# A sparse graph attention kernel: q and softmax weights in columns of their own of two PSUM banks, weights and weighted values one group later

## The chip, the core and the metric

The kernel runs on one core of one Trainium2 chip. Five engines work side by side: TensorE (PE) multiplies matrices and writes only to PSUM, VectorE (DVE) does elementwise work and reductions, ScalarE (ACT) copies and applies functions, GpSimd (POOL) here issues the gathers and takes powers, and SyncE (SP) issues plain DMAs. Each engine runs its own instructions in the program's order and waits on semaphores where it needs another engine's result.

The metric is the device time of the whole kernel in microseconds. The time before is 2392.24 us, the median of three runs from 2391.94 to 2392.58.

## The reference, cut to what matters

Four graph layers over 3327 nodes with 256 features. The adjacency matrix is given densely (3327 x 3327 integers), but a node has only about 16 neighbours. Layer 0 is a small graph attention over the dense matrix. Layers 1 to 3 are alike, each with its own weights: attention of 8 heads over a node's neighbours, then a feed-forward part.

```python
def layer(x, adj, w_qkv, w_proj, b_proj, w1, b1, w2, b2, g1, be1, g2, be2):
    qkv = (layer_norm(x, g1, be1) @ w_qkv).reshape(n, 3, HEADS, HEAD_DIM)
    q, k, v = qkv[:, 0], qkv[:, 1], qkv[:, 2]
    scores = jnp.einsum('nhd,mhd->hnm', q, k) * SCALE
    scores = jnp.where((adj != 0)[None], scores, -jnp.inf)
    attn = jax.nn.softmax(scores, axis=-1)
    out = jnp.einsum('hnm,mhd->nhd', attn, v).reshape(n, DIM)
    x = x + out @ w_proj + b_proj
    ff = jax.nn.gelu(layer_norm(x, g2, be2) @ w1 + b1) @ w2 + b2
    return x + ff
# x = layer 0 of x; then this layer three times, with L1, L2 and L3's weights
```

## The kernel before

**Stages.** The first stage computes layer 0 and, beside it, a list of neighbours for every node. It also sorts the nodes by their number of neighbours, so that a block of 128 nodes has lists of nearly one length. There are 26 blocks; `CAPS` gives each block's list length, from 34 for block 0 down to 9 for block 25. The three attention layers follow. They are written by one function, `layer(L)`, and the order in which instructions stand in each engine's queue is the order of that Python code (`tc.manual_schedule()`).

**A block.** Blocks go through attention in the order 24, 23, ..., 1, 0, 25 (`ORDER`). A block's list is cut into groups of three or four neighbours (`cuts`), so that a block has 3 to 9 groups and a layer 118 groups with 430 neighbours in all. One object of the class `Attend` stands for a block in a layer:

- `gather(g)` (L764) lets GpSimd issue one indirect DMA for each neighbour of a group. It brings the k and v rows of 128 nodes into a slot; there are 12 slots, taken in turn.
- `load_q` (L753) loads the block's q from DRAM through SP's queue (layers 2 and 3), and `place_q` (L757) lets ScalarE copy it into a PSUM tile, `qp`.
- `scores(g)` multiplies the slot's k by q (L778) and sums over each head's 32 columns (L779), both on VectorE.
- `exps` stands after the block's last group: mask and maximum (L785 to L788) on VectorE, and the exponential (L789) on ScalarE.
- `shares` sums the exponentials and inverts the sum (L795, L796), and writes the normalised weights (L799) over q's columns of the same tile `qp`.
- `values(g)` multiplies the slot's v by the weights (L811). TensorE then transposes the products and adds them up in PSUM (L814); after the last group ScalarE copies the result to `oT` (L820).

**The order of the loop.** The loop of `layer` runs over blocks, and within them over groups. In each step it issues gathers up to three groups ahead, this block's scores, one `turn()` of the tails, and then the weighted values of the *block before*: its `shares` in the first group and its groups spread so that they are done one group before this block ends. When the last is done, `place_q` of the next block is issued. It comes so late because q and the weights of a block share columns, and because there are two `qp` tiles: the tile for the next block is the one whose weights have just been used up.

**Tails.** Two blocks together (one for the last two) make a chunk. When a chunk's values are done, a generator `tail` is added to a list, and each `turn()` lets every generator take its next step. A tail is the projection (`pp`, L665) and its residual add (L668), a norm (variance on VectorE, the power L137 on GpSimd, L149 on VectorE, L153 on ScalarE), the transposed input `fT` (L163, L165), the feed-forward in two halves (`pu` L689, gelu L693, `pd` L702), the second residual add (L708), another norm, and the next layer's q, k and v (L183 to L190), which SP writes to DRAM. In the last layer the rows are scattered to the output instead (L713). The list `hidden` lets one tail at a time through its feed-forward.

The tiles `fT` and `hT` of all tails share two buffers. The next layer's gathers can start only when all rows of k and v have been written, so each layer ends with its tails running out while no gather is under way.

Of the kernel before, what the change touches and what calls it, by code (L numbers as in the profile page):

```python
# [8 lines left out]
FP = mybir.dt.float32  # L9
# [6 lines left out]
PSUM = bass.MemoryType.PSUM  # L16
DRAM = bass.MemoryType.DRAM

P = 128
N = 3327  # L20
D = 256
HEADS = 8
# [9 lines left out]
NB = (N + P - 1) // P  # L32
# [10 lines left out]
LW = 40  # L43
# [21 lines left out]
def kernel(ctx: ExitStack, tc: tile.TileContext, ins, out: bass.AP):  # L65
# [563 lines left out]
    with ExitStack() as st:  # L629
# [3 lines left out]
        slots = st.enter_context(tc.tile_pool(name="slots", bufs=SLOTS))  # L633
        ps_g = st.enter_context(tc.tile_pool(name="ps2_g", bufs=4, space=PSUM))
        ps_o = st.enter_context(tc.tile_pool(name="ps2_o", bufs=2, space=PSUM))
        ps_q = st.enter_context(tc.tile_pool(name="ps2_q", bufs=2, space=PSUM))

        def gen(name):
            return ps_g.tile([P, 512], FP, tag="g", name=name)

        x_sb = keep.tile([P, NB, D], FP, name="x_sb")
        def node_x(b):
            nc.scalar.copy(x_sb[:, b, :], nodes_[b][:, :D])

# [7 lines left out]
        def tail(L, w, wqn, blocks, oT):  # L652
# [19 lines left out]
            yield AHEAD - 1  # L672
            xns = normed(work, views, mv, rs, f"f{tag}")
            yield 1
            fT = work.tile([P, 2, 2 * P], FP, tag="fT", name=f"fT_{tag}")
            turned(gen, fT, xns, *gains(L, 1), f"f{tag}")
            yield 1
            pd = None
            while hidden:
                yield 1  # L680
            hidden.append(tag)
            for h in range(2):
                gT = work.tile([P, FH, 2 * P], FP, tag="gT", name=f"gT_{tag}_{h}")
                for f0 in range(0, FH, 2):
# [54 lines left out]
        class Attend:  # L739


            def __init__(self, L, b):
                self.L, self.b, self.tag, self.S = L, b, f"{L}_{b}", CAPS[b]
                self.cuts = cuts(b)
                self.tiles = []
                self.vdone = 0

            def load_q(self):
                if self.L == LAYERS[0]:
# [3 lines left out]
                    nc.sync.dma_start(self.q, q_dr[self.L][:, self.b, :])  # L753

            def place_q(self):
                self.qp = ps_q.tile([P, 512], FP, tag="qp", name=f"qp_{self.tag}")
                nc.scalar.copy(self.qp[:, :D], self.q)  # L757

            def gather(self, g):
                a, z = self.cuts[g]  # L760
# [8 lines left out]
            def scores(self, g):  # L769
                a, z = self.cuts[g]  # L770
                n = z - a
                if g == 0:
                    self.sc = work.tile([P, LW, HEADS], FP, tag="sc", name=f"sc_{self.tag}")
                if self.L == LAYERS[0]:

                    nc.scalar.copy(idx[:, self.b, a:z], self.tiles[g][:, :n, 2 * D])
                kq = self.tiles[g][:, :n, :D]
                nc.vector.tensor_mul(kq, kq, self.qp[:, None, :D].to_broadcast([P, n, D]))  # L778
                nc.vector.tensor_reduce(self.sc[:, a:z, :],  # L779
                                        kq.rearrange("p s (h d) -> p s h d", h=HEADS), AX.X, ALU.add)  # L780

# [9 lines left out]
            def shares(self):  # L791
                S = self.S
                scs = self.sc[:, :S, :]
                sm = work.tile([P, HEADS], FP, tag="sm", name=f"sm_{self.tag}")
                nc.vector.tensor_reduce(sm, scs.rearrange("p s h -> p h s"), AX.X, ALU.add)  # L795
                nc.vector.reciprocal(sm, sm)  # L796

                self.pw = self.qp[:, :LW * HEADS].rearrange("p (s h) -> p s h", h=HEADS)
                nc.vector.tensor_mul(self.pw[:, :S, :], scs, sm[:, None, :].to_broadcast([P, S, HEADS]))  # L799
                self.po = ps_o.tile([P, 2, P], FP, tag="po", name=f"po_{self.tag}")  # L800
                nc.tensor.matmul(self.po.rearrange("p c r -> p (c r)"), zeros_bf[:, :P], zeros_bf,
                                 start=True, stop=False)
# [24 lines left out]
        def turn():  # L827

            for e in list(tails):
                e[0] -= 1  # L830
                if e[0] <= 0:
                    e[0] = next(e[1], None)
                    if e[0] is None:
                        tails.remove(e)

        def layer(L):
            w = load_weights(L)
            wqn = load_wq(L + 1) if L < LAYERS[-1] else None
            att = [Attend(L, b) for b in ORDER]
            todo = [(a, g) for a in att for g in range(len(a.cuts))]  # L840
            turns = len(todo)
            held = 0
            sent = 0
            oTs = {}
            left = [len(c) for c in CHUNKS]
            first = L == LAYERS[0]
            if first:
                for b in ORDER[:EARLY]:
                    node_rows(b)
                    node_x(b)  # L850
            att[0].load_q()
            att[0].place_q()
            att[1].load_q()
            before = None

            def part(a):

                m, j = place[a.b]
                if m not in oTs:
                    oTs[m] = work.tile([P, 2, 2 * P], FP, tag="oT", name=f"oT_{L}_{m}")  # L860
                if a.values(oTs[m], j):
                    left[m] -= 1
                    if not left[m]:
                        tails.append([1, tail(L, w, wqn, CHUNKS[m], oTs.pop(m))])

            now = 0
            for k, a in enumerate(att):
                n = len(a.cuts)
                if k + 2 < NB:
                    att[k + 2].load_q()  # L870
                for g in range(n):
                    if first and g == 0:
                        if k + EARLY < NB:
                            node_rows(ORDER[k + EARLY])
                        if EARLY <= k + 2 < NB:
                            node_list(ORDER[k + 2])
                            node_x(ORDER[k + 2])
                    while sent < turns and held < SLOTS and sent - now <= AHEAD:
                        todo[sent][0].gather(todo[sent][1])
                        sent += 1  # L880
                        held += 1
                    a.scores(g)
                    if g == n - 1:
                        a.exps()
                    turn()
                    if k == NB - 1:
                        turn()
                    if before is not None:
                        if g == 0:
                            before.shares()  # L890
                        goal = max(g + 1, -(-len(before.cuts) * (g + 1) // max(n - 1, 1)))
                        while before.vdone < min(goal, len(before.cuts)):
                            part(before)
                            held -= 1
                            if before.vdone == len(before.cuts) and k + 1 < NB:
                                att[k + 1].place_q()
                    elif g == n - 1:
                        att[1].place_q()
                    now += 1
                before = a  # L900
            before.shares()
            while before.vdone < len(before.cuts):
                part(before)
                turn()
            while tails:
                turn()
# [194 lines left out]
```

## Time and profile before

| what | value |
|---|---|
| median of the runs | 2392.24 us |
| profiled execution | 2871.28 us |
| its span, first to last instruction | 2869.2 us |
| mean granted TensorE clock in it | 0.753 |
| busy: PE, DVE, ACT, POOL | 1716.9, 1756.5, 776.2, 1430.0 us |
| layer 0 and lists, up to the first gather | 411.2 us |
| layer 1, first to last gather | 773.8 us |
| end of layer 1, to the next gather | 77.0 us |
| layer 2, first to last gather | 725.4 us |
| end of layer 2 | 79.2 us |
| layer 3, first to last gather | 734.9 us |
| end of layer 3, to the end | 67.6 us |

A profile shows one execution. In this case it took 479 us longer than the runs without the profiler, so a wait in it isn't at once a wait of the timed runs. In the groups of the page, each line has the source line, the engine, the operation, the tiles written and read, how often; then the busy time and the mean duration, and after the second bar the time for which the engine stood idle just before these instructions, with what ended most of it. "remote" and "another core or an unknown queue" mean that the profile can't name what ended a wait. In a timeline, each row has a start and a duration in us, the engine, the line and the operation, and in brackets the idle time before it.

### The profile page before, as it was taken

Reading aid. Unit: us, or ns where it says so; the run is one execution under the profiler, and the core shown is the slowest. Engines: PE = TensorE matmul, PEld = TensorE weight load, DVE = VectorE, ACT = ScalarE, POOL = GpSimd, SP = SyncE. Lnnn points to the kernel's source line nnn. Section 1 sums busy time; section 2 is a strip of 40 time slices with the busy share of each in tenths; the row PEclk is TensorE's granted clock in tenths of the full one; section 3 lists DMA queues with packets and bytes.
Section 4 is the critical chain, followed back from the end, with each engine's and each line's share of the span. In section 5 each row is a group of like instructions: output and inputs, shape, how many; then the busy total and the mean of one; then the engine's idle time right before and its main releaser. Section 6 shows DMA issues by size and latency. Waiting matters only on the chain.

```text
span 2869.2 us, 26077 instructions
## 1 busy us (share of the span) xinstructions
PE 1716.9 (60%) x8346; PEld 1327.7 (46%) x8346; DVE 1756.5 (61%) x3214; ACT 776.2 (27%) x1564; POOL 1430.0 (50%) x1614
## 2 busy tenths in 40 slices
PE   7677622455666666752576676666725555566556
PEld 6555411444454444642454555554514444444445
DVE  5777735665667776725565755767246467555664
ACT  4777510123322222220232222122302222111112
POOL 0232345554456665336555556664165555665561
PEclk9889855677877667885687777777957777676768
DMA  5667155555456665345545556565255555555451
GB/s 211 218 179 223 59 137 165 151 172 148 129 156 187 178 183 169 109 154 170 148 146 158 174 162 191 169 182 151 99 175 161 155 152 155 168 172 152 145 170 30
DMA packets 165082, 453.04 MB, mean 158 GB/s; under 512 B 37711, under 2 KB 64985, under 8 KB 161609
## 3 DMA queue, kind: packets, MB, share of 16 engines
q0 software_dynamic: 107104, 350.26, 41.8%
q1 hardware_dynamic: 56652, 98.53, 10.9%
q10 hardware_dynamic: 1180, 2.49, 0.3%
q8 instruction: 69, 1.13, 0.2%
q14 instruction: 77, 0.63, 0.1%
HBM read 410.86 MB, written 40.29 MB: 157 GB/s over the span
## 4 chain that ended last, share of the span: by engine, by line
PE 32%; another core or an unknown queue 18%; DVE 17%; issue 15%; ACT 6%; POOL 6%; DMA 5%; DVEq 0%; ACTq 0%; SPq 0%; POOLq 0%
PE pd L702 8%; PE pu L689 7%; PE po L814 5%; PE pk L183 4%; DVE sl L778 4%; DVE sl L811 4%; POOL sl L764 3%; PE pp L665 3%; DVE sc L779 2%; DMA kv<-kvr 2%; DMA sl<-kv,idx 2%; PE pq L188 2%; ACT gT L693 1%; ACT L693 1%
## 5 line engine op out<-in xcount | busy, mean ns | idle before, releaser
L764 POOL DMA_INDIRECT sl<-kv,idx x1290 | 1229.0, 953 | 544.0 <-issue 355.4
L814 PE MATMUL po<-ident,sl 128*128 128x128 f32 x2580 | 471.7, 346 | 568.1 <-DVE sl L811 302.4
L778 DVE TENSOR_TENSOR sl<-sl,qp 128x1024 f32<-128x1024 f32 (+1 forms) x354 | 396.3, 1119 | 568.4 <-ACT qp L757 484.3
L814 PEld LDWEIGHTS po<-ident,sl 128*128 128x128 f32 x2580 | 395.6, 180 | 634.2 <-DVE sl L811 360.3
L702 PE MATMUL pd<-w,gT 128*128 128x256 f32 x1248 | 336.1, 427 | 165.4 <-ACT gT L693 112.6
L779 DVE TENSOR_REDUCE sc<-sl 128x32 f32<-128x1024 f32 (+1 forms) x354 | 398.2, 1125 | 29.5 <-remote 10.5
L689 PE MATMUL pu<-fT,w 128*128 128x256 f32 (+1 forms) x1344 | 328.6, 402 | 127.9 <-issue 66.4
L811 DVE TENSOR_TENSOR sl<-sl,qp 128x1024 f32<-128x1024 f32 (+1 forms) x354 | 388.9, 1119 | 8.1 <-DVE qp L799 3.5
L702 PEld LDWEIGHTS pd<-w,gT 128*128 128x128 f32 x1248 | 261.2, 215 | 228.0 <-ACT gT L693 127.1
L689 PEld LDWEIGHTS pu<-fT,w 128*128 128x128 f32 x1344 | 266.0, 213 | 176.2 <-issue 72.3
L693 ACT ACTIVATE gT<-pu,pv 128x256 f32<-128x256 f32 (+1 forms) x336 | 133.1, 456 | 374.5 <-remote 175.3
L137 POOL TENSOR_TENSOR rsig_f<-rsig_f,mhalf 128x2 f32<-128x2 f32 (+1 forms) x42 | 29.1, 693 | 339.6 <-DVE rsig_f L133 337.6
L820 ACT COPY oT<-po 128x256 f32<-128x256 f32 x78 | 29.1, 373 | 617.3 <-remote 228.6
L183 PE MATMUL pk<-wq,hT 128*128 128x512 f32 x312 | 169.6, 670 | 19.8 <-ACT hT L165 18.6
L708 DVE TENSOR_TENSOR x_sb<-x_sb,pd 128x512 f32<-128x512 f32 (+1 forms) x42 | 27.2, 648 | 207.2 <-PE pd L702 144.9
L608 DVE MAX8 cand<-abf 128x8 f32<-128x256 bf16 x338 | 118.2, 411 | 1.3 <-DMA node<-cand 1.1
L665 PE MATMUL pp<-w_proj,oT 128*128 128x256 f32 x312 | 94.1, 452 | 35.6 <-ACT oT L820 26.3
L165 ACT ACTIVATE fT<-pn_f,pv 128x256 f32<-128x256 f32 (+1 forms) x84 | 41.6, 545 | 249.2 <-remote 155.1
L693 ACT ACT_TABLE_LOAD x48 | 61.6, 1283 | 151.9 <-remote 88.4
L183 PEld LDWEIGHTS pk<-wq,hT 128*128 128x128 f32 x312 | 61.6, 215 | 71.8 <-issue 42.6
L185 ACT COPY kvr<-pk 128x512 f32<-128x512 f32 x78 | 46.0, 589 | 180.5 <-PE pk L183 125.5
L137 POOL TENSOR_TENSOR rsig_h<-rsig_h,mhalf 128x2 f32<-128x2 f32 (+1 forms) x28 | 19.5, 695 | 146.3 <-DVE rsig_h L133 118.2
(220 smaller groups left out, 1999.7 us busy)
## 6 DMA issues: line engine op xcount, KB each, us to landing
a<-in_adj_dram SPq DMA_DIRECT2D x25, 1663.5 KB
sl<-kv,idx POOLq DMA_INDIRECT x1290
kv<-kvr SPq DMA_DIRECT2D x78, 256.0 KB
q<-qr SPq DMA_DIRECT2D x52, 128.0 KB
q<-q SPq DMA_DIRECT2D x52, 128.0 KB
w<-in_L_gnn_w_dram SPq DMA_DIRECT2D x6, 1024.0 KB
node<-x SPq DMA_DIRECT2D x26, 128.0 KB
node<-qr SPq DMA_DIRECT2D x26, 128.0 KB
```

The lines of the kernel that those rows point to most:

```text
L183: nc.tensor.matmul(pk, hT[:, c, :], wq[:, c, D:], start=(c == 0), stop=(c == 1))
L188: nc.tensor.matmul(pq[:, :D], hT[:, c, :], wq[:, c, :D], start=(c == 0), stop=(c == 1))
L608: nc.vector.max(out=cand[:, 8 * m:8 * m + 8], in_=ab3[:, m, :])
L665: nc.tensor.matmul(pp[:, j, :], oT[:, c, j * P:(j + 1) * P], w["w_proj"][:, c, :], start=False, stop=(c == 1 and j == n - 1))
L689: nc.tensor.matmul(pu[:, a, :n * P], w["w1"][:, c, f * P:(f + 1) * P], fT[:, c, :n * P], start=(c == 0), stop=(c == 1))
L693: nc.scalar.activation(gT[:, f0 + a, :n * P], pu[:, a, :n * P], AF.Gelu_apprx_tanh, bias=pv[:, L - 1, 8 + f:9 + f])
L702: nc.tensor.matmul(pd[:, j, :], gT[:, f, j * P:(j + 1) * P], w["w2"][:, h * FH + f, :], start=False, stop=(h == 1 and f == FH - 1 and j == ...
L764: nc.gpsimd.indirect_dma_start(out=t[:, k - a, :w], out_offset=None, in_=kv_dr[self.L][:, :], in_offset=bass.IndirectOffsetOnAxis(ap=idx[: ...
L778: nc.vector.tensor_mul(kq, kq, self.qp[:, None, :D].to_broadcast([P, n, D]))
L779: nc.vector.tensor_reduce(self.sc[:, a:z, :], kq.rearrange("p s (h d) -> p s h d", h=HEADS), AX.X, ALU.add)
L811: nc.vector.tensor_mul(vv, vv, self.pw[:, a:z, :, None].to_broadcast([P, n, HEADS, HD]))
L814: nc.tensor.matmul(self.po[:, c, :], t[:, k, D + c * P:D + (c + 1) * P], ident, is_transpose=True, start=False, stop=(a + k == self.S - 1 ...
```

## The change

There are four edits, which belong together.

1. The two `qp` tiles from a pool become two fixed tiles, `qws`, one PSUM bank each. A block uses one by its place in the order, even or odd. Its q has the first 256 columns and its weights have the last 256 (272 for block 0, whose weights then overlap q's last 16 columns).
2. `place_q` of the block after the next is issued right behind this block's exponentials. The first two blocks' q are placed before the loop.
3. `shares` and `values` of the block before start in the second group of a block, not the first, and end in its last.
4. In `tail`, the wait for `hidden` stands ahead of the making of `fT`, not behind it.

```diff
-        ps_q = st.enter_context(tc.tile_pool(name="ps2_q", bufs=2, space=PSUM))
+        ps_q = st.enter_context(tc.tile_pool(name="ps2_q", bufs=1, space=PSUM))
...
+        qws = [ps_q.tile([P, 512], FP, name=f"qw{k}") for k in range(2)]
...
             xns = normed(work, views, mv, rs, f"f{tag}")
             yield 1
+            while hidden:
+                yield 1
+            hidden.append(tag)
             fT = work.tile([P, 2, 2 * P], FP, tag="fT", name=f"fT_{tag}")
             turned(gen, fT, xns, *gains(L, 1), f"f{tag}")
             yield 1
             pd = None
-            while hidden:
-                yield 1
-            hidden.append(tag)
...
+                w = qws[ORDER.index(b) % 2]
+                self.qp = w[:, :D]
+                self.pw = w[:, 512 - max(D, self.S * HEADS):512].rearrange("p (s h) -> p s h", h=HEADS)
...
             def place_q(self):
-                self.qp = ps_q.tile([P, 512], FP, tag="qp", name=f"qp_{self.tag}")
-                nc.scalar.copy(self.qp[:, :D], self.q)
+                nc.scalar.copy(self.qp, self.q)
...
-                self.pw = self.qp[:, :LW * HEADS].rearrange("p (s h) -> p s h", h=HEADS)
...
             att[1].load_q()
+            att[1].place_q()
...
                     if g == n - 1:
                         a.exps()
+                        if k + 2 < NB:
+                            att[k + 2].place_q()
                     turn()
                     if k == NB - 1:
                         turn()
-                    if before is not None:
-                        if g == 0:
+                    if before is not None and g > 0:
+                        if g == 1:
                             before.shares()
-                        goal = max(g + 1, -(-len(before.cuts) * (g + 1) // max(n - 1, 1)))
+                        goal = max(g, -(-len(before.cuts) * g // (n - 1)))
                         while before.vdone < min(goal, len(before.cuts)):
                             part(before)
                             held -= 1
-                            if before.vdone == len(before.cuts) and k + 1 < NB:
-                                att[k + 1].place_q()
-                    elif g == n - 1:
-                        att[1].place_q()
```

More of the change, by code (lines that the diff above doesn't have):

```diff
@@ L777, in scores @@
                 kq = self.tiles[g][:, :n, :D]
-                nc.vector.tensor_mul(kq, kq, self.qp[:, None, :D].to_broadcast([P, n, D]))
+                nc.vector.tensor_mul(kq, kq, self.qp[:, None, :].to_broadcast([P, n, D]))
                 nc.vector.tensor_reduce(self.sc[:, a:z, :],
```

## The prediction

> **What bounds the kernel now.** I read the times first: the profiled execution took 2871.3 us (span 2869.2), the median without the profiler is 2392.2. The profile is 479 us too long, so before anything is priced I must know what these 479 us are. Then the page's chain and groups, the table by stage, the timeline around the longest wait, and the end of a layer.
>
> The page's chain by engine, and its groups with the gather and the three large VectorE products:
>
> ```profile
> PE 32%; another core or an unknown queue 18%; DVE 17%; issue 15%; ACT 6%; POOL 6%; DMA 5%; DVEq 0%; ACTq 0%; SPq 0%; POOLq 0%
> ...
> L764 POOL DMA_INDIRECT sl<-kv,idx x1290 | 1229.0, 953 | 544.0 <-issue 355.4
> ...
> L778 DVE TENSOR_TENSOR sl<-sl,qp 128x1024 f32<-128x1024 f32 (+1 forms) x354 | 396.3, 1119 | 568.4 <-ACT qp L757 484.3
> L779 DVE TENSOR_REDUCE sc<-sl 128x32 f32<-128x1024 f32 (+1 forms) x354 | 398.2, 1125 | 29.5 <-remote 10.5
> ...
> L811 DVE TENSOR_TENSOR sl<-sl,qp 128x1024 f32<-128x1024 f32 (+1 forms) x354 | 388.9, 1119 | 8.1 <-DVE qp L799 3.5
> ```
>
> The wait that the change goes for is the 484.3 us in the L778 line: VectorE stands until ScalarE has copied the next q into PSUM. It has almost the size of the 479 us, so the timeline of ScalarE, VectorE and GpSimd around one such wait:
>
> ```profile
> 1530.27 1.28 ACT L693 ACT_TABLE_LOAD   x1
> 1547.24 1.57 ACT L693 ACTIVATE gT<-pu,pv 128x256 f32<-128x256 f32 x4 [15.68 <-remote]
> 1548.68 0.39 ACT L820 COPY oT<-po 128x256 f32<-128x256 f32 x1
> 1548.93 0.42 ACT L757 COPY qp<-q 128x256 f32<-128x256 f32 x1
> ...
> 1549.38 1.22 DVE L778 TENSOR_TENSOR sl<-sl,qp 128x1024 f32<-128x1024 f32 x1 [17.05 <-ACT qp L757]
> ...
> 1542.55 0.96 POOL L764 DMA_INDIRECT sl<-kv,idx  x1 [0.30 <-issue]
> 1558.92 0.71 POOL L137 TENSOR_TENSOR rsig_f<-rsig_f,mhalf 128x2 f32<-128x2 f32 x1 [15.42 <-DVE rsig_f L133]
> ```
>
> The q copy (L757) stands behind the copy of the finished rows (L820), and that behind gelus which wait 15.68 us for TensorE. Yet TensorE's rows put the matmuls they wait for at 1528.9 to 1534. Such late signals come about once for each pair of blocks while gathers run; between 1180 and 1290, where they pause, no matmul's signal is over 1 us late. Down the line GpSimd stands 15.42 us at L137 and the gathers with it.
>
> The table by stage (us; busy time of PE, PEld, DVE, ACT, POOL): layer 1, its end, layer 2.
>
> ```profile
> 411.20:1185.00 773.80, 441.13 (x1864) 337.89 (x1864) 507.61 (x963) 179.96 (x479) 445.11 (x473) 0.72 0.56 165
> 1185.00:1262.00 77.00, 64.55 (x330) 48.47 (x330) 31.23 (x61) 28.18 (x68) 4.57 (x7) 0.93 0.13 42
> 1262.00:1987.50 725.50, 441.85 (x1864) 339.11 (x1864) 448.43 (x633) 159.28 (x317) 424.39 (x452) 0.74 0.59 175
> ```
>
> Now GpSimd's sum. Gathers that follow without a wait start every 1.257 us (0.95 busy, 0.30 to the next). The three layers last 773.8, 725.4 and 734.9 us from first to last gather: 2234.1. In them GpSimd must do 3 x 429 steps of 1.257 = 1617.8; 55 powers (L137) of 0.71 with a 0.19 gap = 50; 22 row gathers of layer 1 (L199) at 1.25 = 28; 22 output scatters of layer 3 at 1.3 plus the 22.7 us that they wait for each other's landing = 51. Together 1746, so in the profile it stands 488 us. Without them the profiled execution would take 2871 - 488 = 2383 us, 9 below the median. My reading: in the timed runs the late signals are mostly gone and **GpSimd's gather queue sets the pace inside the layers**; VectorE (448 of 725 us busy in layer 2) follows with room. The 484 us are mainly the profiler's.
>
> **What the Trainium skill says.** "Perfetto Trace Analysis", section "Tensor Engine Instruction (MATMUL, LD_WEIGHTS)": a matmul's reported end is computed from its size, the signal comes later. The trace agrees: end at 1534, gelus at 1547.24. "DMA: Bandwidth & Descriptors", section "SWDGE vs HWDGE vs iDMA": descriptors of irregular DMAs are computed by software on GpSimd; this agrees with a gather that costs 0.95 us of that engine whoever waits, and I take its price to be the same without the profiler. "PSUM — Partial Sum Buffer", section "Terms": two engines may not use one bank at once, so q's copy and the weights of one bank have to be ordered even in separate columns; the trace only shows copy and product in turn. "ScalarE: Activation LUTs", section "Terms": a table load is about 2.7 us; here it is 1.28 (L789, L693), and the trace decides.
>
> **The change part by part.**
>
> *q placed earlier.* The 78 copies of 0.38 us stay. Each moves from behind the last weighted values (and L820) of the block before to right behind the exponentials, one block earlier than it is read. L778 then never waits for TensorE by way of L820. The new cover is a whole block, 12 us for the smallest. On SP the q load stays at the block's start; in layers 2 and 3 it must land before the copy at the block's end, or ScalarE's later gelus stand behind it; 28.7 us of such waits in 2 cases now. I take 0, bound 0 to +10.
>
> *Weights one group later.* L795, L796, L799 (0.36 + 0.20 + 0.30) wait for the exponential, which may have a 1.28 us table load ahead; with one more group of scores (2.4 us) between, that is covered. If TensorE is late, nothing of this helps L668 and L708, the residual adds (91.5 and 144.9 us of waits in the profile): they are next.
>
> *Values one group later.* Same products, same transposes. A slot is held one group (5 us) longer. A gather's slot is that of 12 groups before; with blocks of 6 groups its values come 7 groups after its scores, so 4 groups remain: 0, bound +5.
>
> *Where VectorE's delay counts.* Inside layers only the 9 us. At the end of a layer its lateness is on the path: the first group of the last block of layer 1 is scored 12 us after its last gather is issued, at the layer's start it is 4, so 8 us are late, 3 x 8 = 24 with three layers. 9 + 24 = 33 us at most; I take 30.
>
> *What the layer's end loses.* There the tails run one after another:
>
> ```profile
> 1225.71 0.69 DVE L708 TENSOR_TENSOR x_sb<-x_sb,pd 128x512 f32<-128x512 f32 x1 [7.84 <-PE pd L702]
> ...
> 1240.48 0.42 DVE L708 TENSOR_TENSOR x_sb<-x_sb,pd 128x256 f32<-128x256 f32 x1 [10.32 <-PE pd L702]
> ...
> 1250.72 0.42 DVE L708 TENSOR_TENSOR x_sb<-x_sb,pd 128x256 f32<-128x256 f32 x1 [8.04 <-PE pd L702]
> ```
>
> Three feed-forwards follow each other, then the kv rows are written and the next layer's gather starts at 1262.07. With values one group later each starts later. Of the last pair, the 32 transposes of four groups (3.66 us) now lie between its first pu and pd, where they ended before pu; pu itself starts some 2 us earlier, so +1.6. The next block's L149 comes behind the last block's L668 and statistics (0.42 + 0.43 + 0.18 + 0.15 = 1.2). And fT is now made after the place is free (`hidden`): a transpose of 0.38 and an activation of 0.81, +1.2. That is +4; where VectorE is not late, the whole group of 5 us shows and it is about +10. I take 6 a layer: +18.
>
> Sum: 2392.2 - 30 + 18 = **2380 us**. In the profiled execution more can come off, as late signals no longer reach VectorE by L757; that is not in the timed runs.
>
> **The rivals.**
> 1. *Much faster: the queue has more room than I think.* If the 0.30 us gap is 0.19 without the profiler (the gap after L137), the queue needs 1290 x 0.11 = 142 us less and stands that much for VectorE. L757's share of VectorE's waits is 484 of some 820 us; 59% of 142 is 84, half of it 42; with the 18 back, 2392 - 42 + 18 = 2368, with all 2326; I put it at 2345. For it: the size of the wait. Against: the 2383 fit the median almost by themselves.
> 2. *Slower: the layer's end.* VectorE isn't late in the timed runs, nothing is won there, and each end costs 6 to 10 us: +18 to +30, less up to 9 won inside: 2412. One place (TensorE's order between last gather and first of the next layer), one price, and it decides as soon as less than 18 us are won. For it: the gathers need no VectorE that is faster. Against: the lags of 12 us.
> 3. *The wait only moves.* The copy now shares a bank with weights that L799 is to write; if L799 waits for it uncovered, 78 x 0.4 = 31 us on VectorE, which it has room for: 2392, no change.
>
> **How the numbers follow.** Forecast 45%, own range 2365 to 2396; rival 1 22% (2320 to 2365), rival 2 29% (2397 to 2425), rival 3 4%. About 0.2% (5 us) is what can be told from no change. Of the forecast's 45, some 28 lie below 2387.5, 11 within 0.2%, 6 above. Faster: 28 and 21 of rival 1, 49; same: 11 and 1, 2 and 3 of the rivals, 17; slower: 6, 27 of rival 2 and 1 of rival 3, 34. Range 2338 to 2418: it leaves some 15 in 100 out.
>
> **What would show it.** Right: no L778 wait on L757; gathers at 1.257 us still; a shorter lag of scores behind gathers at the layers' ends; ends of 70 to 80 us. Wrong: ends over 83 us (rival 2), or a gather pitch that doesn't fit the new median (rival 1), or new waits at L799 on L757 (rival 3).

## The result and the profile after

The changed kernel takes 2420.98 us, the median of four runs (2420.44 to 2428.16), against 2392.09 us for the kernel before, measured beside it (four runs, 2391.92 to 2392.58). The ratio is 1.0142, 95% interval 1.0122 to 1.0163; the quotient of the two medians is 1.0121. It is 29 us slower, where 2380 us were predicted.

The runs were made in series, each on one chip, and the series met one of two conditions. In some, TensorE's signals came late while gathers were being issued: the kernel before then has medians of 2868 to 2894 us (single runs 2863 to 2915), with a granted clock of about 0.75. In others they did not: medians of 2385 to 2392 us (single runs 2383 to 2401), clock about 0.79. I call them the late and the undisturbed condition. What sets them isn't known; it is not the chip alone, since one chip met the late condition in one series (e1 to e4) and, within the hour, the undisturbed in another (p1 to p4). "Late" is said against the end that the trace gives for a matmul; whether the matmul or only its signal is late, the traces don't tell.

The result above was taken undisturbed, and so was the profile after; the profile before, which the prediction read, was of the late condition. The fair comparison is therefore with a trace of the kernel before that was taken undisturbed in the last series (f1 below, in which no matmul's signal is over 1 us late). One trace is one run: f1's took 2395.47 us where its series has a median of 2389.10, and that of the changed kernel 2428.16 where the median is 2420.98. The first stage alone, which no edit touches, takes 416 to 428 us in the eight undisturbed traces. So traces are compared by stages below, and not by their whole time.

The page of the changed kernel: its chain by engine, and the groups of the gather, of the first VectorE product and of the second residual add.

```profile
PE 34%; DVE 22%; DMA 15%; POOL 13%; issue 11%; ACT 4%; DVEq 0%; POOLq 0%; ACTq 0%; SPq 0%
...
L769 POOL DMA_INDIRECT sl<-kv,idx x1290 | 1229.8, 953 | 437.6 <-issue 308.2
...
L783 DVE TENSOR_TENSOR sl<-sl,qw 128x1024 f32<-128x1024 f32 (+1 forms) x354 | 396.2, 1119 | 197.7 <-DMA sl<-kv,idx 115.4
...
L711 DVE TENSOR_TENSOR x_sb<-x_sb,pd 128x512 f32<-128x512 f32 (+1 forms) x42 | 27.2, 647 | 191.2 <-PE pd L705 191.1
```

The 18% under "another core or an unknown queue" are gone, and a gather costs what it did, 953 ns. The wait on q's copy has left the first product's line, but for the starts of layers 2 and 3 (44.4 us); the largest wait of VectorE is now for `pd`, at the residual add. The same two products and the add in the undisturbed kernel before:

```profile
L778 DVE TENSOR_TENSOR sl<-sl,qp 128x1024 f32<-128x1024 f32 (+1 forms) x354 | 396.8, 1121 | 252.0 <-DMA sl<-kv,idx 148.5
...
L708 DVE TENSOR_TENSOR x_sb<-x_sb,pd 128x512 f32<-128x512 f32 (+1 forms) x42 | 27.2, 648 | 135.7 <-PE pd L702 135.7
```

So undisturbed there never were 484 us to win at L778: 252.0 us in all, 88.6 of them put down to L757 by the list of waits, and some of those put down to the gathers (148.5) are L757's too, as one case below shows.

Both traces cut at each layer's first and last gather, in us (first column from the start to the first gather; the last end runs to the kernel's end):

| | start | layer 1 | its end | layer 2 | its end | layer 3 | its end | sum |
|---|---|---|---|---|---|---|---|---|
| before (f1) | 424.9 | 594.0 | 78.2 | 561.4 | 75.8 | 599.2 | 59.9 | 2393.4 |
| after | 424.4 | 601.8 | 78.2 | 572.6 | 78.8 | 598.2 | 72.3 | 2426.3 |
| difference | -0.5 | +7.8 | 0.0 | +11.2 | +3.0 | -1.0 | +12.4 | +32.9 |

Two places pay about the same: the inside of layers 1 and 2 (+19.0, layer 3 gives 1.0 back) and the ends (+15.4, most of it behind layer 3).

### The profile page after: what moved, and what is told of

The parts are those of the page before. It is cut to its first block, busy times and chain, and to the rows that moved or that the text cites. A ratio compares the mean times of both kernels' runs of the same rounds, so it can differ in the third digit from the quotient of the medians.

```text
span 2426.3 us, 26146 instructions
## 1 busy us (share of the span) xinstructions
PE 1666.4 (69%) x8346; PEld 1310.2 (54%) x8346; DVE 1756.7 (72%) x3214; ACT 780.1 (32%) x1564; POOL 1431.0 (59%) x1614
## 4 chain that ended last, share of the span: by engine, by line
PE 34%; DVE 22%; DMA 15%; POOL 13%; issue 11%; ACT 4%; DVEq 0%; POOLq 0%; ACTq 0%; SPq 0%
DMA sl<-kv,idx 11%; POOL sl L769 9%; PE pd L705 8%; PE pu L692 7%; PE po L817 6%; DVE sl L783 5%; PE pk L183 5%; DVE sl L814 4%; DVE sc L784 3%; DMA kv<-kvr 2%; PE pq L188 2%; PE pp L668 2%; DVE cand L608 1%; DVE st_f L130 1%; POOL out_dram L716 1%
## 5 line engine op out<-in xcount | busy, mean ns | idle before, releaser
L817 PE MATMUL po<-ident,sl 128*128 128x128 f32 x2580 | 476.8, 350 | 545.5 <-DVE sl L814 544.8
L817 PEld LDWEIGHTS po<-ident,sl 128*128 128x128 f32 x2580 | 401.2, 183 | 613.4 <-DVE sl L814 602.6
L783 DVE TENSOR_TENSOR sl<-sl,qw 128x1024 f32<-128x1024 f32 (+1 forms) x354 | 396.2, 1119 | 197.7 <-DMA sl<-kv,idx 115.4
L784 DVE TENSOR_REDUCE sc<-sl 128x32 f32<-128x1024 f32 (+1 forms) x354 | 398.2, 1125 | 12.1
L814 DVE TENSOR_TENSOR sl<-sl,qw 128x1024 f32<-128x1024 f32 (+1 forms) x354 | 389.2, 1119 | 2.7
L692 PE MATMUL pu<-fT,w 128*128 128x256 f32 (+1 forms) x1344 | 306.0, 384 | 7.9 <-ACT fT L165 7.9
L705 PE MATMUL pd<-w,gT 128*128 128x256 f32 x1248 | 297.0, 392 | 6.4 <-ACT gT L696 6.4
L692 PEld LDWEIGHTS pu<-fT,w 128*128 128x128 f32 x1344 | 253.9, 204 | 44.2 <-ACT fT L165 12.6
L705 PEld LDWEIGHTS pd<-w,gT 128*128 128x128 f32 x1248 | 238.0, 196 | 48.1 <-ACT gT L696 11.0
L711 DVE TENSOR_TENSOR x_sb<-x_sb,pd 128x512 f32<-128x512 f32 (+1 forms) x42 | 27.2, 647 | 191.2 <-PE pd L705 191.1
L794 ACT ACTIVATE sc<-sc 128x120 f32<-128x120 f32 (+11 forms) x78 | 24.4, 313 | 384.9 <-DVE sc L793 354.8
L598 ACT ACTIVATE aT<-pt 128x1024 bf16<-128x1024 bf16 x104 | 85.8, 871 | 8.3 <-PE pt L597 8.0
L188 PEld LDWEIGHTS pq<-wq,hT 128*128 128x128 f32 x312 | 62.4, 200 | 47.0 <-issue 39.6
```

Source lines behind the costliest of these rows:

```text
L188: nc.tensor.matmul(pq[:, :D], hT[:, c, :], wq[:, c, :D], start=(c == 0), stop=(c == 1))
L692: nc.tensor.matmul(pu[:, a, :n * P], w["w1"][:, c, f * P:(f + 1) * P], fT[:, c, :n * P], start=(c == 0), stop=(c == 1))
L705: nc.tensor.matmul(pd[:, j, :], gT[:, f, j * P:(j + 1) * P], w["w2"][:, h * FH + f, :], start=False, stop=(h == 1 and f == FH - 1 and j == ...
L783: nc.vector.tensor_mul(kq, kq, self.qp[:, None, :].to_broadcast([P, n, D]))
L784: nc.vector.tensor_reduce(self.sc[:, a:z, :], kq.rearrange("p s (h d) -> p s h d", h=HEADS), AX.X, ALU.add)
L814: nc.vector.tensor_mul(vv, vv, self.pw[:, a:z, :, None].to_broadcast([P, n, HEADS, HD]))
```

## The experiments

The expectations weigh two theories: "ends" has the 29 us lost between a layer's last gather and the next layer's first, "inside" has them lost between a layer's first and last gather.

### First in the late condition

The first three series met the late condition. The expectations of the first two still reckon with 2392 us, so their absolute numbers miss by a fifth and only ratios and stages can be compared. The kernel before, for its trace in each series:

> The kernel before, unchanged, to see a second profile of it. Both theories expect a time of 2392 us. If the late TensorE signals of the first profile were a chance of that one execution, this profile spans about 2390 us and shows the gather queue without the 488 us of standing; if the profiler brings them out each time in this kernel, it spans about 2870 us again.

> The kernel before on another chip, for a profile without late TensorE signals. If such signals belong to a chip and not to the profiler, a chip that runs this kernel in 2392 us also profiles it at about 2392. Then theory ends: the three layers last from first to last gather what they last in the changed kernel (602, 573 and 598 us within 10), and the three ends are 8 to 12 us shorter than its 78, 79 and 72. Theory inside: the ends are equal within 3 us and the layers are shorter by 29 us in all.

> The kernel before, once more, to have its trace beside that of the changed kernel on one chip. If this chip is one on which TensorE's signals come late while gathers are issued: about 2892 us, layers of 774, 735, 734 us from first to last gather, ends of 76, 78, 67 us. If it is one on which they do not: about 2392 us, and then the trace settles where the 29 us of the change lie. Theory 'ends' (the prediction's second rival): ends of about 68 to 70 us each, 20 to 30 us less in sum than the 229 us of the changed kernel, and 25 to 30 us of standing gather queue inside layers 1 and 2 as in the changed kernel. Theory 'inside': ends of 76, 78, 67 us as in the disturbed trace, and less than 10 us of standing queue inside the layers.

It took 2903.08, 2894.09 and 2876.79 us, with ends of 76 to 77, 77 to 78 and 67 us. None of them gave the undisturbed trace that was wanted. What they do show is that the 479 us of the first profile weren't the profiler's: runs of the kernel before that were only timed took as long (medians 2892.47 of 27, 2894.17 of 32, 2868.46 of 4).

The changed kernel itself, in the third series; and, once in each of the three, a kernel with all edits but the last block's share of edit 3:

> The changed kernel unchanged, beside the kernel before on this chip. With late signals: faster than before by 1.5 to 2.5 per cent (2820 to 2850 us), as the same kernel with the last block's values at their old place was (0.976 to 0.979 there), with ends 3 to 5 us longer each than that kernel's 74, 75, 65 us. Without late signals: 1.012 to 1.016 times before, ends 78, 79, 72 us.

```diff
-                    if before is not None and g > 0:
-                        if g == 1:
+                    late = 1 if k < NB - 1 else 0
+                    if before is not None and g >= late:
+                        if g == late:
                             before.shares()
-                        goal = max(g, -(-len(before.cuts) * g // (n - 1)))
+                        d = g + 1 - late
+                        goal = max(d, -(-len(before.cuts) * d // (n - 1)))
```

> The changed kernel, but in a layer's last block the weights and values of the block before start in the first group again. Theory ends: part of the 29 us comes back, 4 to 6 us at each of three ends, so 2403 to 2410 us, with the three ends shorter by as much and the layers' insides unchanged. Theory inside: within 3 us of the changed kernel's 2421.

> The changed kernel with the last block's schedule as before, on this chip. Theory ends: 10 to 20 us below the changed kernel (2401 to 2411 us where that takes 2421), all of it between a layer's last gather and the next layer's first. Theory inside: within 3 us of the changed kernel.

> The changed kernel with values of the last block starting in its first group, as before the change. With late signals: 0.976 to 0.979 times before again. Without late signals: theory 'ends' has it back at the time of before within 8 us, since only the layers' ends differ (ends 4 to 7 us shorter each than the changed kernel's would leave it at 1.004 to 1.008); theory 'inside' has it at 1.010 to 1.014, with the standing of the gather queue in layers 1 and 2 unchanged at about 29 us.

The changed kernel took 0.9783 times before (0.9683 to 0.9883; two runs against four): the same change that loses over 1% undisturbed wins 2% when signals are late, from 2868.46 to 2812.01 us. The other kernel took 0.9787, 0.9757 and 0.979 times before, with ends 5.1, 4.2 and 6.9 us shorter than those of the changed kernel in the third series; its whole time there was the same, 2814.06 us. VectorE's longest waits in the trace of before and of the changed kernel in that series (e9, e10; total us, times, longest):

```profile
DVE sl L778 <- ACT qp L757: 464.4, 35, 23.5
DVE x_sb L708 <- PE pd L702: 147.1, 27, 17.0
DVE x_sb L668 <- PE pp L665: 77.6, 25, 7.0
```

```profile
DVE x_sb L671 <- PE pp L668: 309.7, 24, 29.2
DVE x_sb L711 <- PE pd L705: 238.9, 25, 20.8
```

Of the 464.4 us that VectorE stood for q's copy, 324 reappear at the two residual adds (309.7 - 77.6 and 238.9 - 147.1). So in VectorE's queue TensorE's lateness is for the most part only met further down; where the 2% come from is seen in GpSimd's waits, under "Where the time went".

Single edits in the same condition: edit 4 alone, and edits 1 and 2 alone (values and `hidden` as before).

> The kernel before with edit 4 alone: fT is made after the place in the feed-forward is free. Theory ends (the 29 us are lost between a layer's last gather and the next layer's first): one exposed transpose and activation of fT for one or two tails at each end, 3 x 1.2 to 2.4, so 2396 to 2399 us. Theory inside (the feed-forwards start later in the layers, VectorE waits longer at the residual adds, and the gathers stand at L137): most of the 29 us, 2410 us or more.

> Edit 4 alone, on this chip. Theory ends: 2396 to 2399 us, the ends longer by 1 to 3 us each. Theory inside: 2410 us or more.

> The kernel before with edits 1 and 2 alone: q and weights in columns of their own, q placed two blocks ahead; weights and values as before. Theory ends: nothing is lost, 2385 to 2393 us. Theory that the early copy of q costs (ScalarE waits for q's load, or the weights wait for the copy): 2400 us or more. The forecast's step that VectorE's lateness at the layers' ends is won back would give 2370 to 2380.

> Edits 1 and 2 alone, on this chip. Theory ends: 2385 to 2393 us, nothing lost and nothing won. Theory that the early copy costs: 2400 us or more.

Edit 4 did nothing: 1.0000 (0.9967 to 1.0033) and 0.9999 (0.9971 to 1.0026). Edits 1 and 2 cost a little: 1.0032 (1.0008 to 1.0056) and 1.0041 (1.0015 to 1.0067). So the 2% don't come without edit 3, the one that was not aimed at a wait. Edit 3 alone wasn't tried, so whether it needs the others is open. (Without edit 4, by my reading of the code, it could wait in a circle, since `fT` and `hT` of all tails share two buffers.)

### VectorE without a backlog at a layer's end

To read the ends apart from VectorE's backlog, GpSimd was made to hold the last block's gathers until VectorE has multiplied the group ahead of them. The small product (L137's operand `mhalf`) is there only for its wait:

```diff
+                    if k == NB - 1 and g == 0:
+                        seen_ = small.tile([P, 6], FP, tag="st", name=f"seen_{L}")
+                        nc.gpsimd.tensor_tensor(seen_[:, :2], before.tiles[-1][:, 0, :2], mhalf[:, :2], ALU.mult)
-                    while sent < turns and held < SLOTS and sent - now <= AHEAD:
+                    while (sent < turns and held < SLOTS and sent - now <= AHEAD
+                           and (k == NB - 1 or todo[sent][0] is not att[-1])):
```

> The kernel before, in which GpSimd issues the last block's gathers only after VectorE has multiplied the k of the group ahead of them: VectorE enters the layer's end with no backlog, as it does in the changed kernel's first profile (4 to 9 us behind the last block's first gathers, against 12 to 19 in the disturbed trace of before). Only the time from a layer's last gather to the next one counts here, not the whole time. Theory 'ends' (the second rival): that time falls by 5 to 9 us an end, to about 69, 70, 61 us, since before's ends of 77, 78, 68 contained VectorE's backlog. Theory 'inside': it stays at 75 to 78, 76 to 79, 66 to 69.

> The changed kernel with the same pause ahead of the last block. Both theories: ends as in its first profile, 78, 79, 72 us, since VectorE had little backlog there. Theory 'ends': so 20 to 28 us more in sum of three than the kernel before with the pause; theory 'inside': no more than 12 us more in sum.

> The kernel before with edit 4 alone (fT made after its place is free) and the pause. If the late fT is part of the end's price, 1 to 3 us an end more than the kernel before with the pause; by the step of the prediction, 1.2 us of each tail that waits for its place, up to 3.6 an end. If not, within 1 us.

> The changed kernel with the last block's hand-over to values at its old place, and the pause. Theory 'ends', with the later values of the second last block as the cause: 4 to 7 us an end less than the changed kernel with the pause, so at the kernel before with the pause plus at most edit 4's share. Theory 'inside': no difference over 2 us an end, once VectorE has no backlog.

This series met the undisturbed condition (before without the pause: 2385.22 us). Every kernel ran once. Ends by stage, in us:

| with the pause | end 1 | end 2 | end 3 | sum | whole time |
|---|---|---|---|---|---|
| before (p1) | 68.7 | 67.1 | 64.0 | 199.8 | 2394.18 |
| edit 4 alone (p3) | 69.5 | 67.3 | 63.7 | 200.5 | 2397.69 |
| changed, last block as before (p4) | 70.8 | 70.8 | 65.3 | 206.9 | 2412.74 |
| changed (p2) | 77.5 | 75.8 | 70.7 | 224.0 | 2432.63 |

With VectorE in the same state the change costs 24.2 us at the ends, as the theory "ends" had it. The later `fT` has no part in it (+0.7), against the prediction's 1.2 us a tail; the last block's later values have 17.1, and the rest of the order about 6. Inside the layers p2 takes 6.1 us more than p1, but the pause's own waits are 19.5 us in p1 and 7.6 in p2; without them it is 18.0 more, as in the traces without the pause.

### The undisturbed kernel before, and what is left of each place

> The kernel before, unpaused, for its trace without late signals: 2385 to 2392 us; ends of about 69, 68, 64 us as with the pause, no wait of L778 on L757 over 5 us, and about 20, 5 and 0 us of standing gather queue in layers 1, 2, 3, so that ends give 20 to 26 of the 29 us of the changed kernel and the inside of layers 3 to 9. (If TensorE's signals come late in this call, 2868 to 2892 us, and it says nothing on this.)

The expectation missed at the ends: they are 78.2, 75.8 and 59.9 us, not 69, 68 and 64, and so the ends have 15.4 us of the change's price, not 20 to 26. The last block's first group is scored 11 us after its last gather was issued in layers 1 and 2, and 4 us in layer 3. So without any late signal VectorE does enter the ends of layers 1 and 2 with a backlog of 7 us, and that of layer 3 with none. Neither theory alone holds. The pause had taken that backlog away in layers 1 and 2 (9.5 and 8.7 us), and cost 4.1 us in layer 3.

The next kernel keeps edit 3 out of the last two blocks, where the kernel of the late series kept it out of the last alone:

```diff
-                    late = 1 if k < NB - 1 else 0
+                    late = 1 if k < NB - 2 else 0
```

> The changed kernel with the values of the two blocks before the last at their old place (the last two blocks take them over in their first group), so that only the inner blocks have the later values. If the rest of the ends' price (6 us beyond the last block's share) is from block 0's group: 1.002 to 1.005 times before without late signals, ends of 69, 69, 65 us; if it is from the inner order: 1.006 to 1.009. With late signals: 0.976 to 0.982 in both cases.

It took 1.0028 times before (1.0015 to 1.0042; 2396.21 against 2389.10 us as medians, 20 and 31 runs). Its ends are 68.8, 69.6 and 60.2 us, so the last two blocks hold the whole price of the ends; the last block's first group is scored 5, 6 and 4 us after its last gather, not 11, 11 and 4. Its layers are not better than the changed kernel's: 603.3, 575.0 and 599.1 us.

> Edits 1 and 2 alone (q and weights in columns of their own, q placed one block earlier). Prediction's step: 0, bound 0 to +10 us, so 1.000 to 1.004 times before, with ends as before within 2 us: then the 29 us are all of the later values. A rival: q's copy right behind the exponentials, with the wait for its load in ScalarE's queue, costs 5 us and more: 1.002 to 1.004 with ScalarE's waits on q's load grown. With late signals: 1.003 to 1.004.

This kernel, edits 1 and 2 alone, took 1.0006 times before (0.9988 to 1.0024), with layers of 596.3, 562.4 and 597.8 us and ends of 75.5, 75.6 and 59.2. Edits 1 and 2 cost nothing that can be told from chance; with edit 4 inert (p3's layers are within 1.2 us of p1's), neither price, inside or at the ends, comes without edit 3. By VectorE's waits in layer 2, edits 1 and 2 alone already move the wait: first the kernel before (f1), then f3.

```profile
DVE sl L778 <- ACT qp L757: 48.3, 7, 23.6
DVE x_sb L708 <- PE pd L702: 30.8, 10, 9.4
```

```profile
DVE x_sb L711 <- PE pd L705: 62.3, 10, 10.4
DVE sl L783 <- ACT qw L762: 23.6, 1, 23.6
```

One wait of 23.6 us stays at L762: it is the layer's start. The other 24.7 us left that line, and 31.5 came to the residual add.

## Where the time went

**Inside layers 1 and 2: the slots.** GpSimd's waits in layer 2, from first to last gather, before (f1) and after:

```profile
POOL sl L764 <- PE po L814: 3.8, 5, 1.8
```

```profile
POOL sl L769 <- PE po L817: 17.0, 12, 3.7
```

A gather's slot is free when TensorE has transposed the values of 12 groups before. These sums hold the usual gap of 0.30 us between two gathers as well; and in layer 1 a part of such waits stands under other names. So here are all of GpSimd's waits of over 0.45 us inside the three layers, by what stood waiting, in us:

| | powers (L137) | gathers | scatters | sum | layers 1 to 3 |
|---|---|---|---|---|---|
| before (f1) | 14.7 | 6.4 | 27.3 | 48.4 | 1754.6 |
| edits 1 and 2 (f3) | 19.2 | 5.7 | 26.0 | 50.9 | 1756.5 |
| changed, last two blocks as before (f2) | 11.8 | 35.8 | 25.8 | 73.4 | 1777.4 |
| changed | 8.4 | 35.1 | 24.5 | 68.0 | 1772.5 |
| late: before (e9) | 329.3 | 147.8 | 57.6 | 534.7 | 2226.1 |
| late: changed (e10) | 234.2 | 207.1 | 30.0 | 471.3 | 2157.6 |

Undisturbed, the gathers wait 35 us with edit 3 and 6 without it, and the layers grow by about what the sum grows. The same trade is a gain in the late condition: 59 us more at the gathers, but 95 less at the powers and 28 less at the scatters. Undisturbed there is little at the powers to win. Why the powers are ready sooner is not shown.

In the changed kernel these waits, all but 2.8 us, stand ahead of the first gather of the same groups in both layers: groups 65, 75, 85, 95, 100 and 106, counted from 0, with 3.5, 3.5, 1.6, 4.2, 1.6 and 2.8 us in layer 1 and 3.0, 3.0, 1.0, 3.7, 2.5 and 2.0 in layer 2. In layer 1 the trace puts three of them down to L783 and one to L781; but all, save those of group 100, end 1.9 to 2.8 us after VectorE has ended the v product (L814 there, in `values`) of 12 groups before, whatever name they stand under. (At group 100 of layer 2 it is 7.7 us, and the transposes came last.) One pair of blocks in layer 2, GpSimd before and after:

```profile
1541.60 0.72 POOL L137 TENSOR_TENSOR rsig_h<-rsig_h,mhalf 128x2 f32<-128x2 f32 x1 [2.48 <-DVE rsig_h L133]
1543.83 0.70 POOL L137 TENSOR_TENSOR rsig_f<-rsig_f,mhalf 128x2 f32<-128x2 f32 x1 [1.51 <-DVE rsig_f L133]
1544.70 1.02 POOL L764 DMA_INDIRECT sl<-kv,idx  x1 [0.17 <-issue]
```

```profile
1558.79 0.72 POOL L137 TENSOR_TENSOR rsig_h<-rsig_h,mhalf 128x2 f32<-128x2 f32 x1 [1.31 <-DVE rsig_h L133]
1560.96 0.70 POOL L137 TENSOR_TENSOR rsig_f<-rsig_f,mhalf 128x2 f32<-128x2 f32 x1 [1.44 <-DVE rsig_f L133]
1565.36 1.02 POOL L769 DMA_INDIRECT sl<-kv,idx  x1 [3.71 <-PE po L817]
```

Before, the gather behind the powers (the first of group 94) follows at once, and so does the first of group 95. After, the gather behind the powers is the first of group 95, and it waits 3.71 us for a slot. Over that time VectorE's rows show why the slot isn't free, before and after:

```profile
1536.55 0.95 DVE L778 TENSOR_TENSOR sl<-sl,qp 128x768 f32<-128x768 f32 x1 [7.76 <-DMA sl<-kv,idx]
1537.54 0.95 DVE L779 TENSOR_REDUCE sc<-sl 128x24 f32<-128x768 f32 x1
1539.33 0.69 DVE L708 TENSOR_TENSOR x_sb<-x_sb,pd 128x512 f32<-128x512 f32 x1 [0.83 <-PE pd L702]
```

```profile
1556.52 0.69 DVE L711 TENSOR_TENSOR x_sb<-x_sb,pd 128x512 f32<-128x512 f32 x1 [8.95 <-PE pd L705]
...
1561.84 1.22 DVE L814 TENSOR_TENSOR sl<-sl,qw 128x1024 f32<-128x1024 f32 x1
```

The first wait is put down to a gather, but that group's gathers were issued from 1513.2 to 1515.7, some 21 us earlier. ScalarE's row in the same trace names what really came last, q's copy:

```profile
1536.14 0.38 ACT L757 COPY qp<-q 128x256 f32<-128x256 f32 x1
```

So VectorE stands 7.76 us before and 8.95 us after at this place, while TensorE works through the tails; only the stand has moved from the head of a block to the residual add. In layers 1 and 2 the lag of scores behind the issue of their group's last gather rises to 27.1 and 25.1 us before, 25.9 and 24.1 after. That is five groups of four gathers (5 us each), and with the six or seven groups from scores to values they use up the 12 slots.

How little room that left is seen in the kernel before. At groups 65, 75, 85 and 95 a gather starts 2.7 to 4.8 us after the v product of 12 groups before has ended; where gathers wait for this, in the changed kernel, it is 1.9 to 2.8. So values one group (5 us) later had at most 3 us of room. In layer 3 of the kernel before the lag stays under 10 us and that time is 22 us and more; there the change cost nothing (-1.0). That the slots are the cause is read from the traces; a 13th slot would test it and wasn't tried.

**At the ends: TensorE's order.** TensorE at the end of layer 3, before (f1, last gather at 2333.5) and after (last gather at 2354.0); start, duration, idle time ahead:

```profile
2336.99 0.93 PE L163 MATMUL pn_f<-ident,xn_f 128*128 128x128 f32 x4 [1.51 <-ACT xn_f L153]
2337.76 4.16 PE L814 MATMUL po<-ident,sl 128*128 128x128 f32 x32
2341.75 3.62 PE L689 MATMUL pu<-fT,w 128*128 128x256 f32 x16
...
2346.89 3.72 PE L702 MATMUL pd<-w,gT 128*128 128x256 f32 x16
...
2362.26 2.18 PE L689 MATMUL pu<-fT,w 128*128 128x128 f32 x16 [0.55 <-ACT fT L165]
```

```profile
2358.21 7.02 PE L817 MATMUL po<-ident,sl 128*128 128x128 f32 x36 [17.01 <-DVE sl L814]
2365.06 0.60 PE L163 MATMUL pn_f<-ident,xn_f 128*128 128x128 f32 x4
2366.32 3.74 PE L692 MATMUL pu<-fT,w 128*128 128x256 f32 x16 [0.66 <-ACT fT L165]
2369.90 3.66 PE L817 MATMUL po<-ident,sl 128*128 128x128 f32 x32
...
2374.82 3.72 PE L705 MATMUL pd<-w,gT 128*128 128x256 f32 x16
...
2391.44 0.69 PE L163 MATMUL pn_f<-ident,xn_f 128*128 128x128 f32 x2 [2.14 <-ACT xn_f L153]
2392.68 3.79 PE L692 MATMUL pu<-fT,w 128*128 128x128 f32 x16 [0.55 <-ACT fT L165]
```

Counted from the last gather, `pu` of the last pair starts at 8.3 us before and 12.3 after, because 36 transposes now stand ahead of the pair's `pn_f`, behind an idle stretch of 17.01 us. The next 32 transposes, which lay ahead of `pu`, lie between `pu` and `pd`: the pair's first `pd` is at 13.4 and 20.8. Its residual add is at 25.7 and 34.1 us, the next block's at 36.6 and 49.0. VectorE at the pair's add, before and after:

```profile
2359.23 0.69 DVE L708 TENSOR_TENSOR x_sb<-x_sb,pd 128x512 f32<-128x512 f32 x1 [7.85 <-PE pd L702]
2359.83 0.15 DVE L149 SCALAR_TENSOR_TENSOR nmu_f<-mv_f,rsig_f 128x1 f32<-128x1 f32 x1
```

```profile
2388.07 0.69 DVE L711 TENSOR_TENSOR x_sb<-x_sb,pd 128x512 f32<-128x512 f32 x1 [6.07 <-PE pd L705]
2389.34 0.42 DVE L671 TENSOR_TENSOR x_sb<-x_sb,pp 128x256 f32<-128x256 f32 x1 [0.58 <-PE pp L668]
...
2390.55 0.15 DVE L149 SCALAR_TENSOR_TENSOR nmu_f<-mv_f,rsig_f 128x1 f32<-128x1 f32 x1
```

The steps are 4.1, 3.3 and 0.9 us up to the pair's add. Then 1.9: L149 stands behind the next block's L671 and its statistics, and starts 2.5 us after the pair's add, not 0.6. And 2.2 us come with slower matmuls: the first 16 of the next `pu` take 3.79 us, not 2.18. From there on both kernels take the same 23.3 us.

The granted clock (the third number from the right) in the stretches from 0 to 16 us and from 35 to 50 us after the last gather of the changed kernel:

```profile
2354.00:2370.00 16.00, 11.14 (x57) 10.33 (x58) 13.98 (x20) 3.95 (x7) 1.68 (x2) 0.68 0.12 39
...
2389.00:2404.00 15.00, 11.76 (x57) 9.72 (x55) 1.83 (x7) 5.17 (x14) 2.88 (x4) 0.77 0.05 17
```

In the kernel before it is 1.00 all through this end. The Trainium skill, "TensorE: Matmul & The Clock Gate", section "Part 1: The HAM clock gate", has the clock fall to half after about 3.4 us of idling. The traces agree that a stand is followed by the half clock, but the 3.4 us aren't borne out: by the trace's clock record the clock was halved 2.4 us after TensorE stopped (at 2343.6, in the stand of 17.01 us), and at 2391.4 with the end of a stand of 2.14 us.

## Right and wrong, by the prediction's own steps

The predicted sum was -30 for VectorE's lateness (of at most 24 at the ends and 9 inside; I put it as 24 and 6) and +18 for the ends. By the three traces f1, f2 and after, one of each kernel (f3's ends, of a kernel level with before, are up to 2.7 us from f1's, so that much can be chance):

| term | predicted | measured |
|---|---|---|
| lateness that the ends lose (f2 - f1) | -24 | -15.3 |
| inside the layers (after - f1) | -6 | +18.0 |
| what an end pays (after - f2) | +18 | +30.7 |
| start | 0 | -0.5 |
| sum | -12 | +32.9 |

- **Wrong, and the step that failed most: "so 4 groups remain: 0, bound +5" for the values one group later.** The four groups were counted and taken as free. The count left out how far the gathers run ahead of the scores: in layers 1 and 2 up to 27 and 25 us, five groups, so that at most 3 us of room were left where 5 were needed. The gathers' waits inside the layers grew from 6.4 to 35.1 us. The waits for powers fell by 6.3 us, about the 6 that were to be won inside (or only because GpSimd now comes later); in all the inside lost 18.
- **Wrong in size: "what the layer's end loses", 6 us each.** By after minus f2 it was 9.4, 9.2 and 12.1, the prediction's own "about +10". Its parts: "pu itself starts some 2 us earlier" came out 4.1 later at layer 3; the 32 transposes between `pu` and `pd` came as said (3.3); L149 behind L671 came as said (1.9 against 1.2); `fT` after `hidden` cost nothing (1.2 predicted); the slower clock (2.2) wasn't in the sum.
- **Right in kind, too large: VectorE's lateness at the ends.** Read in one layer and multiplied by three. It is there in layers 1 and 2 even undisturbed (9.4 and 6.2 us won in f2), and absent in layer 3. The lag of 12 us was read in a trace whose late signals the prediction itself held to be missing in the timed runs; that it came out at 11 in two layers of an undisturbed trace was luck.
- **Wrong: "the 484 us are mainly the profiler's".** They belonged to a condition of the machine in which timed runs are as long. The conclusion drawn from it, that the timed runs to be predicted were free of them, held for the runs that gave the result, and 2383 us, reckoned without the waits, was close. In the late condition the change won 2%, more than the forecast.
- **Right: the gather queue.** The pitch is 1.257 to 1.260 us on average in every trace, and layers 1 to 3 undisturbed (1754.6 us) are close to the 1746 us that GpSimd must do.
- **The rivals.** Rival 2 (2412, own range 2397 to 2425) named the sign and one of the two places; that its range holds 2421 is in part luck, since it put the inside at nothing or a gain. Its test, ends over 83 us, didn't show: ends of 78.2, 78.8 and 72.3 hid the price under the vanished backlog. Rival 3's move of the wait happened, but to L711 and L671, not to L802; by f3 it was free, as that rival had it, and the price came with the later values. Nothing was seen for rival 1: GpSimd's gap between gathers stayed at 0.30 us.

No kernel here beats the one before in the undisturbed condition; q placed early without edit 3 is level with it. In the late condition the changed kernel is 2% faster. The kernel of f2, 0.3% slower undisturbed, wasn't run there.

## What to carry to other kernels

Before a wait in a profile is priced, ask whether the profiled execution and the timed runs are of one kind. If they differ by as much as the wait is large, a second trace of the same kernel is worth more than an argument on whose the difference is. When a consumer is moved later, don't only count the buffers: read in a trace, in the middle of the work, how long a buffer has been free when it is filled again. And read the price of a drain at the last stage, where nothing hides it.

## What the runs showed of the hardware

- The same program had medians of 2385 to 2392 us or of 2868 to 2894 us, 20% apart, each steady within about 1.5% over up to 32 runs of a series, and both on one chip. In the late traces some 850 to 940 us are covered by matmuls whose signal came over 1 us after the end on record, in 125 to 153 episodes; in the undisturbed ones there is none. None of these matmuls ends in the first stage or between the layers, where no gathers are issued.
- In the late condition a change can win what it loses in the other: 0.978 against 1.014 times before for one kernel. What it traded, GpSimd's waits at the powers against those at the gathers, was 329 and 148 us in the one condition and 15 and 6 in the other.
- 16 matmuls of 128 columns took 3.79 us behind a stand of TensorE of 2.14 us, with the clock at half up to 2398.3, where the same 16 took 2.18 us at full clock in the kernel before.
- A gather of 128 rows took 0.953 us of GpSimd and a pitch of 1.257 to 1.260 us in both conditions.
